# A 409.6 MB score matrix in wider stores: memory by parts of 1024 rows in groups of six

## The chip, the cores and the metric

The kernel runs on one core of one Trainium2 chip. The metric is the device time of a run in microseconds, median of several runs. Before the change it is 1660.91 us (three runs, 1660.71 to 1662.82). A separate run under the hardware profiler took 1589.44 us; all views below are of that run, whose span from the first to the last instruction is 1587.5 us.

## The reference

1024 sequences of 50 item numbers select rows of an embedding table of 100001 x 128 floats (row 0 counts as zero). Running means over time are normalised over the batch, drive a spiking neuron for 50 steps, and the mean spike rate is multiplied with the whole table:

```python
e = emb[seq]                                   # 1024 x 50 x 128
prefix = jnp.cumsum(e, axis=1)
denom = jnp.minimum(t_idx[None, :], lengths[:, None])
uF = prefix / denom[:, :, None]
y = (uF - uF.mean(axis=0)) * lax.rsqrt(uF.var(axis=0) + BN_EPS) * gamma + beta
def step(v, x):
    v = v + (x - v) / TAU                      # TAU = 2
    spike = atan_spike(v - V_TH)               # 1 where v >= 1
    v = v - lax.stop_gradient(spike) * V_TH
    return (v, spike)
_, spikes = lax.scan(step, v0, x_seq)
uF_out = spikes.mean(axis=0)                   # 1024 x 128
scores = uF_out @ emb.T                        # 1024 x 100001 floats, 409.6 MB
```

## The kernel before

There are two stages. In the first, GpSimd gathers 1024 table rows for each of 50 steps, and the other engines turn, normalise and integrate them; the table's first rows are loaded beside that. The result is the spike counts, `counts[n]`, eight blocks of 128 sequences. In the second, the table is worked through in chunks of 4096 rows, each of four parts of 1024 rows. A part is transposed on TensorE, split in two halves of reduced precision (`hi`, `lo`) by ScalarE and VectorE, multiplied with each of the eight blocks, evicted from PSUM in turn by VectorE and ScalarE into an output tile of 16 KB per partition, and stored.

The load of a chunk; eight chunks (32 parts) are loaded at the start from the SP queue, later ones from the ScalarE queue:

```python
CH = 4096
AHEAD = 8
HALF = 1024
...
def fetch(c, pool):
    engine = nc.sync if c < AHEAD else nc.scalar
    c0, w = chunks[c]
    r = pool.tile([P, CH // P, D], F32, tag="rows", name=f"rows_{c}")
    whole = w // HALF
    if whole:
        engine.dma_start(
            out=r[:, : whole * KQ, :].rearrange("p (q k) d -> p q (k d)", q=whole),
            in_=table[c0 : c0 + whole * HALF, :].rearrange("(q p k) d -> p q (k d)", p=P, k=KQ),
        )
    ...
```

Transposing and splitting a part, the product, the store:

```python
def turned(c, q, pt):
    ...
    for k0 in range(0, hw, P):
        nc.tensor.transpose(pt[:, k0 : k0 + kw], rows[c][:kw, q * KQ + k0 // P, :], ident[:kw, :kw])

def upper(c, q, pt):
    ...
    nc.scalar.copy(vh, vp)

def lower(c, q, pt):
    ...
    nc.vector.tensor_tensor(vl, vp, vh.bitcast(F32), ALU.subtract)

def product(po, c, q, n, k0, kw):
    for j, part in enumerate(split[c, q][:2]):
        nc.tensor.matmul(po[:, :kw], lhsT=counts[n], rhs=part[:, k0 : k0 + kw], start=j == 0, stop=j == 1)

def store(n, c0, o):
    nc.sync.dma_start(out=out[n * P : (n + 1) * P, c0 : c0 + o.shape[1]], in_=o)
```

The second stage (block 0 of the first chunk is done while the first stage ends):

```python
op = ctx.enter_context(tc.tile_pool(name="o", bufs=3, reuse_waits="tile"))
...
for c, (c0, w) in enumerate(chunks):
    todo = [(c + 1, q) for q in range(parts[c + 1])] if c + 1 < len(chunks) else []

    def ready():
        if todo and free:
            i, q = todo.pop(0)
            prepare(i, q, psum.tile([P, HALF], F32, tag="ps", name=f"pt_{i}_{q}"))

    for n in range(NB):
        ...
        o = op.tile([P, CH], F32, tag="o", name=f"o_{c}_{n}")
        for q in range(parts[c]):
            ...
            po = psum.tile([P, HALF], F32, tag="ps", name=f"po_{c}_{n}_{q}")
            for k0 in range(0, hw, BANK):
                product(po[:, k0 : k0 + BANK], c, q, n, k0, min(BANK, hw - k0))
            if turn % 2 == 0:
                nc.vector.tensor_scalar_mul(o[:, h0 : h0 + hw], po[:, :hw], 1.0 / T)
            else:
                nc.scalar.mul(o[:, h0 : h0 + hw], po[:, :hw], 1.0 / T)
            turn += 1
            ...
            if n == NB - 1:
                free.append(split.pop((c, q))[2])
                ready()
        if c or n > 1:
            store(n, c0, o[:, :w])
        if n in (2, 5):
            ready()
    if c + 2 == AHEAD:
        more = extrap.tile([P, 4, HALF], F32R, tag="rows", name="more")
        free += [(None, (more[:, i, :], more[:, i + 1, :])) for i in (0, 2)]
    elif ahead:
        fetch(ahead.pop(0), rowp)
```

`free` is the list of places for split parts: four at first, a fifth when the second stage begins, seven from the seventh chunk on.

Of the kernel before, what the change touches and what calls it, by code (L numbers as in the profile page):

```python
# [12 lines left out]
F32 = mybir.dt.float32  # L13
# [7 lines left out]
P = 128  # L21
BN_EPS = 1e-5
V_TH = 1.0
CH = 4096
AHEAD = 8
HALF = 1024
KQ = HALF // P
BANK = 512


@with_exitstack
def rec_kernel(
# [17 lines left out]

    const = ctx.enter_context(tc.tile_pool(name="const", bufs=1))
    embp = ctx.enter_context(tc.tile_pool(name="embT", bufs=1))
    rowp = ctx.enter_context(tc.tile_pool(name="rows", bufs=AHEAD - 2))

    extrap = ctx.enter_context(tc.tile_pool(name="extra", bufs=1))


    countA = const.tile([P, P], F32R, tag="countA", name="countA")
# [6 lines left out]

    chunks = [(c0, min(CH, N - c0)) for c0 in range(0, N, CH)]
    rows = {}
    split = {}  # L70
    parts = [-(-w // HALF) for _, w in chunks]

    free = [(embp, i) for i in range(4)]

    def fetch(c, pool):

        engine = nc.sync if c < AHEAD else nc.scalar
        c0, w = chunks[c]
        r = pool.tile([P, CH // P, D], F32, tag="rows", name=f"rows_{c}")
        whole = w // HALF  # L80
        if whole:
            engine.dma_start(
                out=r[:, : whole * KQ, :].rearrange("p (q k) d -> p q (k d)", q=whole),
                in_=table[c0 : c0 + whole * HALF, :].rearrange("(q p k) d -> p q (k d)", p=P, k=KQ),
            )
        c1 = c0 + whole * HALF
        full, rest = divmod(w - whole * HALF, P)
        k0 = whole * KQ
        if full:
            engine.dma_start(  # L90
                out=r[:, k0 : k0 + full, :],
                in_=table[c1 : c1 + full * P, :].rearrange("(k p) d -> p k d", p=P),
            )
        if rest:
            engine.dma_start(out=r[:rest, k0 + full, :], in_=table[c1 + full * P : c0 + w, :])
        rows[c] = r

    def turned(c, q, pt):
        hw = min(HALF, chunks[c][1] - q * HALF)
        if c == 0 and q == 0:  # L100
            nc.vector.memset(rows[c][0:1, 0, :], 0.0)
        for k0 in range(0, hw, P):
            kw = min(P, hw - k0)
            nc.tensor.transpose(pt[:, k0 : k0 + kw], rows[c][:kw, q * KQ + k0 // P, :], ident[:kw, :kw])  # L104

    def slot(c, q):
        place = free.pop(0)
        pool, i = place
        if pool is None:
            hi, lo = i  # L110
        else:
            hi = pool.tile([P, HALF], F32R, tag=f"hi{i}", name=f"hi_{c}_{q}")
            lo = pool.tile([P, HALF], F32R, tag=f"lo{i}", name=f"lo_{c}_{q}")
        split[c, q] = hi, lo, place
        return hi, lo

    def views(c, q, pt, hi, lo):
        hw = min(HALF, chunks[c][1] - q * HALF)
        if hw < HALF:
            return pt[:, :hw], hi[:, :hw], lo[:, :hw]  # L120
        return (
            pt.rearrange("d (k p) -> d p k", k=KQ),
            hi.rearrange("d (p k) -> d p k", k=KQ),
            lo.rearrange("d (p k) -> d p k", k=KQ),
        )

    def upper(c, q, pt):
        hi, lo = slot(c, q)  # L130
        hw = min(HALF, chunks[c][1] - q * HALF)
        if hw % 2:
            nc.vector.memset(hi[:, hw : hw + 1].bitcast(F32), 0.0)
            nc.vector.memset(lo[:, hw : hw + 1].bitcast(F32), 0.0)
        vp, vh, vl = views(c, q, pt, hi, lo)
        nc.scalar.copy(vh, vp)  # L136

    def lower(c, q, pt):
        vp, vh, vl = views(c, q, pt, *split[c, q][:2])
        nc.vector.tensor_tensor(vl, vp, vh.bitcast(F32), ALU.subtract)  # L140

    def prepare(c, q, pt):
        turned(c, q, pt)
        upper(c, q, pt)
        lower(c, q, pt)

    def product(po, c, q, n, k0, kw):
        kw += kw % 2  # L150
        for j, part in enumerate(split[c, q][:2]):
            nc.tensor.matmul(  # L152
                po[:, :kw],
                lhsT=counts[n],
                rhs=part[:, k0 : k0 + kw],
                start=j == 0,
                stop=j == 1,
            )
# [3 lines left out]


    with ExitStack() as ph:
        row0p = ph.enter_context(tc.tile_pool(name="rows0", bufs=1))
        once = ph.enter_context(tc.tile_pool(name="once", bufs=1))
        lp = ph.enter_context(tc.tile_pool(name="lif", bufs=2))
        sp = ph.enter_context(tc.tile_pool(name="stats", bufs=3))
# [11 lines left out]
        gb = once.tile([P, 2], F32, tag="gb", name="gb")  # L180
        nc.sync.dma_start(out=gb[:, 0:1], in_=gamma.rearrange("(d o) -> d o", o=1))
        nc.sync.dma_start(out=gb[:, 1:2], in_=beta.rearrange("(d o) -> d o", o=1))
        for c in range(min(AHEAD, len(chunks))):
            fetch(c, row0p if c == 0 else extrap if c == AHEAD - 1 else rowp)

        es = {}

# [99 lines left out]
        for t in range(T):  # L287
# [62 lines left out]
            if not last:  # L350
# [5 lines left out]
                if t + 2 < T:  # L356
                    l = only(t + 2)

                if T - 8 <= t < T - 2 and t % 2 == 0:
                    q = (t - T + 8) // 2  # L360
                    prepare(0, q, vp.tile([P, HALF], F32, tag="v1", name=f"pt_{q}"))

        pt = vp.tile([P, HALF], F32, tag="v0", name="pt_3")
        turned(0, 3, pt)
        x(halves[0])
        x(halves[1])
        upper(0, 3, pt)
        step(halves[0])  # L370
        spiked(countA, slice(0, P), vt)


        o = gp.tile([P, HALF], F32, tag="e", name="o_0_0_0")
        for h, po in enumerate(pre):
            product(po, 0, 0, 0, h * BANK, BANK)
        step(halves[1])
        nc.scalar.mul(o[:, :BANK], pre[0], 1.0 / T)
        store(0, 0, o[:, :BANK])
        lower(0, 3, pt)  # L380
        nc.vector.tensor_scalar_mul(o[:, BANK:], pre[1], 1.0 / T)
        store(0, BANK, o[:, BANK:])
        spiked(countB, slice(P, BANK), vt)
        spiked(countC, halves[1], vt)
        for q in range(1, 4):
            pool, tag = (gp, "e") if q == 1 else (up, "uF")
            o = pool.tile([P, HALF], F32, tag=tag, name=f"o_0_0_{q}")
            if q == 1:
                po = sums
            else:  # L390
                po = vp.tile([P, HALF], F32, tag=f"v{(q + 1) % 2}", name=f"po_0_0_{q}")
                po = [po[:, cs] for cs in halves]
            for h, cs in enumerate(halves):
                product(po[h], 0, q, 0, h * BANK, BANK)
            nc.scalar.mul(o[:, :BANK], po[0], 1.0 / T)
            nc.vector.tensor_scalar_mul(o[:, BANK:], po[1], 1.0 / T)
            store(0, q * HALF, o)

    embp2 = ctx.enter_context(tc.tile_pool(name="embT2", bufs=1, reuse_waits="tile"))
    op = ctx.enter_context(tc.tile_pool(name="o", bufs=3, reuse_waits="tile"))
    psum = ctx.enter_context(
        tc.tile_pool(name="psum", bufs=4, space=bass.MemoryType.PSUM, reuse_waits="tile")
    )
    free.append((embp2, 4))
    turn = 0
    ahead = list(range(AHEAD, len(chunks)))

    for c, (c0, w) in enumerate(chunks):
        todo = [(c + 1, q) for q in range(parts[c + 1])] if c + 1 < len(chunks) else []

        def ready():
            if todo and free:
                i, q = todo.pop(0)
                prepare(i, q, psum.tile([P, HALF], F32, tag="ps", name=f"pt_{i}_{q}"))

        for n in range(NB):
            if c == 0 and n == 0:  # L420
                continue
            if c + 1 < len(chunks):
                o = op.tile([P, CH], F32, tag="o", name=f"o_{c}_{n}")
            else:

                o = rowp.tile([P, CH], F32, tag="rows", name=f"o_{c}_{n}")
            for q in range(parts[c]):
                h0 = q * HALF
                hw = min(HALF, w - h0)
                po = psum.tile([P, HALF], F32, tag="ps", name=f"po_{c}_{n}_{q}")  # L430
                for k0 in range(0, hw, BANK):
                    product(po[:, k0 : k0 + BANK], c, q, n, k0, min(BANK, hw - k0))
                if turn % 2 == 0:
                    nc.vector.tensor_scalar_mul(o[:, h0 : h0 + hw], po[:, :hw], 1.0 / T)  # L434
                else:
                    nc.scalar.mul(o[:, h0 : h0 + hw], po[:, :hw], 1.0 / T)  # L436
                turn += 1
                if c == 0 and n == 1 and q % 2:
                    store(n, c0 + h0 - HALF, o[:, h0 - HALF : h0 + HALF])
                if n == NB - 1:  # L440
                    free.append(split.pop((c, q))[2])
                    ready()
            if c or n > 1:
                store(n, c0, o[:, :w])
            if n in (2, 5):
                ready()
        assert not todo
        if c + 2 == AHEAD:
            more = extrap.tile([P, 4, HALF], F32R, tag="rows", name="more")
            free += [(None, (more[:, i, :], more[:, i + 1, :])) for i in (0, 2)]  # L450
        elif ahead:
            fetch(ahead.pop(0), rowp)


# [17 lines left out]
```

## Time and profile before

| | |
|---|---|
| time, median of 3 | 1660.91 us |
| profiled span | 1587.5 us |
| mean granted TensorE clock | 0.954 |
| HBM read / written | 77.69 MB / 409.60 MB |
| stores of 2048 KB | 190, median 12.8 us from issue to landing |
| loads of 2048 KB on the ScalarE queue | 16, median 27.0 us to landing |
| ScalarE evictions that waited for a store to land | 347.4 us in 134 waits |
| VectorE evictions that waited for a store to land | 338.5 us in 136 waits |

How to read the views quoted below: a page gives each engine's busy time with its share of the span; then the span in 40 slices, in which a digit is the busy share in tenths; then the DMA queues (q1 is the SP queue's, q10 the ScalarE queue's, q0 the gathers') with packets, megabytes and the share of 16 DMA engines' time; then the chain of work that ended last, as shares of the span. An eviction that waits for a store costs nothing by itself: it shows that the output tiles are full, and the question is what the stores wait for.

### The profile page before, as it was taken

To read this page: it belongs to the slowest core of one execution; us is meant where nothing else is said; L and a number is where in the kernel's file an instruction comes from. 1 tells how busy PE (TensorE), PEld (TensorE's weight loads), DVE (VectorE), ACT (ScalarE), POOL (GpSimd) and SP (SyncE) were. 2 spreads that over 40 slices of the span, in tenths; PEclk is the share of its full clock that TensorE was granted. 3 is DMA by queue.
4 is the path that set the end of the run, shared out by engine and by line. 5 is a ranking of instruction groups with operands and counts; after the bars stand their busy time and mean duration, and the time that the engine had idled before them with its cause. 6 is when DMAs were issued, how large, how long until landed. Compare 5 with 4: busy or idle time off the path is not lost.

```text
span 1587.5 us, 12689 instructions
## 1 busy us (share of the span) xinstructions
PE 1137.8 (72%) x4532; PEld 804.7 (51%) x4532; DVE 939.4 (59%) x1162; ACT 631.6 (40%) x699; POOL 378.4 (24%) x406
## 2 busy tenths in 40 slices
PE   4555555555555977788888878788888788888884
PEld 2222222222233765566666666666666666666663
DVE  4777777777778654555555554555555545555553
ACT  2322222222233544444444444444444444444442
POOL 6777777777775000000000000000000000000000
PEclk9999999999965999999999999999999999999998
DMA  9522122221221999999999999999999999999998
GB/s 341 187 53 53 52 53 53 53 53 52 53 53 51 380 429 426 424 422 415 418 426 407 418 426 422 417 414 415 416 416 419 422 420 411 427 411 412 416 417 345
DMA packets 58410, 488.13 MB, mean 307 GB/s; under 512 B 12491, under 2 KB 13292, under 8 KB 33772
## 3 DMA queue, kind: packets, MB, share of 16 engines
q1 hardware_dynamic: 36256, 426.67, 63.9%
q0 software_dynamic: 12800, 26.24, 6.1%
q10 hardware_dynamic: 9292, 34.42, 6.1%
q8 instruction: 35, 0.57, 0.1%
q14 instruction: 27, 0.22, 0.0%
HBM read 77.69 MB, written 409.60 MB: 307 GB/s over the span
## 4 chain that ended last, share of the span: by engine, by line
DMA 52%; POOL 18%; issue 10%; PE 9%; DVE 7%; ACT 3%; DVEq 0%; SPq 0%; ACTq 0%; POOLq 0%
DMA scores<-o 48%; POOL e L191 18%; PE po L152 8%; DVE o L434 5%; DMA e<-in_L_rec_emb_table,idx 3%; ACT o L436 3%; PE pt L104 1%; PE pre L300 0%; ACT hi L136 0%; DVE s L330 0%; DVE bs L310 0%; DVE uF L309 0%; DMA idx<-in_r_seq 0%; ACT v L345 0%; DVE negv L353 0%
## 5 line engine op out<-in xcount | busy, mean ns | idle before, releaser
L434 DVE TENSOR_SCALAR o<-po 128x1024 f32<-128x1024 f32 x390 | 462.6, 1220 | 442.0 <-DMA scores<-o 338.5
L436 ACT ACTIVATE o<-po 128x1024 f32<-128x1024 f32 (+1 forms) x390 | 385.4, 1018 | 528.2 <-DMA scores<-o 347.4
L191 POOL DMA_INDIRECT e<-in_L_rec_emb_table,idx x400 | 377.7, 944 | 124.6 <-issue 116.4
L152 PE MATMUL po<-hi,countC 128*128 128x512 f32 x624 | 261.0, 418 | 81.7 <-ACT o L436 81.5
L300 PE MATMUL pre<-ident,e 128*128 128x128 f32 x400 | 155.9, 451 | 146.9 <-DMA e<-in_L_rec_emb_table,idx 145.0
L152 PE MATMUL po<-lo,countC 128*128 128x512 f32 x624 | 248.9, 399 | 0.0
L152 PE MATMUL po<-hi,countB 128*128 128x512 f32 x468 | 192.2, 411 | 14.4 <-ACT o L436 13.9
L300 PEld LDWEIGHTS pre<-ident,e 128*128 128x128 f32 x400 | 79.2, 200 | 241.7 <-DMA e<-in_L_rec_emb_table,idx 219.9
L152 PEld LDWEIGHTS po<-hi,countC 128*128 128x128 f32 x624 | 120.2, 193 | 133.5 <-ACT o L436 110.7
L152 PE MATMUL po<-lo,countB 128*128 128x512 f32 x468 | 186.9, 399 | 0.0
L104 PE MATMUL pt<-ident,rows 128*128 128x128 f32 x782 | 113.2, 292 | 70.5 <-ACT o L436 65.4
L104 PEld LDWEIGHTS pt<-ident,rows 128*128 128x128 f32 x782 | 96.4, 150 | 96.3 <-ACT o L436 79.8
L324 ACT ACTIVATE r<-mv,eps 128x1 f32<-128x1 f32 x50 | 14.8, 295 | 302.8 <-DVE mv L320 302.8
L152 PEld LDWEIGHTS po<-lo,countC 128*128 128x128 f32 x624 | 120.5, 193 | 22.1
L309 DVE SCALAR_TENSOR_TENSOR uF<-rlen,pre 128x512 f32<-128x512 f32 x100 | 68.3, 683 | 105.5 <-PE pre L300 105.5
L140 DVE TENSOR_TENSOR lo<-pt,hi 128x1024 fp32r<-128x1024 f32 x78 | 93.7, 1218 | 40.9 <-ACT hi L136 40.9
L152 PEld LDWEIGHTS po<-hi,countB 128*128 128x128 f32 x468 | 91.6, 196 | 41.7 <-ACT o L436 19.8
L152 PEld LDWEIGHTS po<-lo,countB 128*128 128x128 f32 x468 | 91.1, 195 | 18.2
L152 PE MATMUL po<-more,countC 128*128 128x512 f32 (+1 forms) x320 | 87.7, 413 | 16.1 <-ACT o L436 16.1
L136 ACT CAST hi<-pt 128x1024 fp32r<-128x1024 f32 x78 | 79.0, 1013 | 48.7 <-PE pt L104 48.7
L268 PE MATMUL sums<-s,ident_h 128*128 128x512 bf16 x98 | 49.6, 608 | 61.1 <-DVE s L330 61.1
L257 PE MATMUL pre<-zT,l 128*128 128x512 f32 x100 | 76.9, 771 | 19.7 <-DVE uF L309 19.5
(77 smaller groups left out, 942.7 us busy)
## 6 DMA issues: line engine op xcount, KB each, us to landing
scores<-o SPq DMA_DIRECT2D x190, 2048.0 KB, 12.8
rows<-in_L_rec_emb_table ACTq DMA_DIRECT2D x16, 2048.0 KB, 27.0
rows<-in_L_rec_emb_table SPq DMA_DIRECT2D x8, 2048.0 KB, 26.0
scores<-o SPq DMA_DIRECT2D x8, 848.5 KB, 14.6
e<-in_L_rec_emb_table,idx POOLq DMA_INDIRECT x400, 2.5
scores<-o SPq DMA_DIRECT2D x2, 1024.0 KB, 3.9
scores<-o SPq DMA_DIRECT2D x3, 512.0 KB, 2.7
scores<-o SPq DMA_DIRECT2D x2, 256.0 KB, 2.1
```

The costliest lines, as they stand in the source:

```text
L104: nc.tensor.transpose(pt[:, k0 : k0 + kw], rows[c][:kw, q * KQ + k0 // P, :], ident[:kw, :kw])
L136: nc.scalar.copy(vh, vp)
L140: nc.vector.tensor_tensor(vl, vp, vh.bitcast(F32), ALU.subtract)
L152: nc.tensor.matmul(po[:, :kw], lhsT=counts[n], rhs=part[:, k0 : k0 + kw], start=j == 0, stop=j == 1,)
L191: nc.gpsimd.indirect_dma_start(out=es[t][:, n * P : (n + 1) * P], out_offset=None, in_=table, in_offset=bass.IndirectOffsetOnAxis(ap=idx[: ...
L257: nc.tensor.matmul(pre[h], lhsT=l, rhs=zT[:, h * BANK : (h + 1) * BANK], start=t == 0, stop=False, skip_group_check=True,)
L268: nc.tensor.matmul(sums[h], lhsT=ident_h, rhs=s[:, h * BANK : (h + 1) * BANK], start=t == 0, stop=t == T - 2, skip_group_check=True,)
L300: nc.tensor.matmul(pre[h][:, k : k + P], lhsT=e[:, h * BANK + k : h * BANK + k + P], rhs=ident, start=False, stop=last, is_transpose=True, ...
L309: nc.vector.scalar_tensor_tensor(uF[:, cs], rlen[:, cs], 1.0 / (t + 1), pre[h], ALU.max, ALU.mult)
L324: nc.scalar.activation(r, mv[:, 1:2], AF.Sqrt, bias=eps)
L434: nc.vector.tensor_scalar_mul(o[:, h0 : h0 + hw], po[:, :hw], 1.0 / T)
L436: nc.scalar.mul(o[:, h0 : h0 + hw], po[:, :hw], 1.0 / T)
```

## The change

The unit of memory becomes the part of 1024 rows instead of the chunk of 4096. Loads come in groups of six parts; six groups (36 parts instead of 32) are brought in during the first stage. The second stage's chunks are 2, 2, 2, 3, 3, 3, 3, then twelve times 6, then 4, 4 parts wide. Memory that earlier groups leave becomes places for split parts (ten in the end, instead of seven) and output tiles (three of 24 KB per partition instead of three of 16 KB). It is for longer rows in each store, for fewer loads beside the stores, and for more room to split parts ahead of their use. The diff, cut to what matters:

```diff
-CH = 4096
-AHEAD = 8
+GROUP = 6
+AHEAD = 6
+
+WIDTHS = [2, 2, 2, 3, 3, 3, 3] + 12 * [6] + [4, 4]
+NARROW, MIDDLE = 3, 7
...
+    free = [
+        [embp.tile([P, HALF], F32R, tag=f"{x}{i}", name=f"{x}_{i}") for x in ("hi", "lo")] for i in range(2)
+    ]
+    def group(g):
+        at = g if g < AHEAD else AHEAD - 2 + g % 2
+        r = rowp.tile([P, GROUP, HALF], F32, tag=f"rows{at}", name=f"rows_{g}")
+        for k in range(GROUP):
+            rows[g * GROUP + k] = r[:, k, :]
+        return r
...
-        for c in range(min(AHEAD, len(chunks))):
-            fetch(c, row0p if c == 0 else extrap if c == AHEAD - 1 else rowp)
+        for g in range(AHEAD):
+            fetch(group(g), g * GROUP, GROUP)
...
-                if T - 8 <= t < T - 2 and t % 2 == 0:
+                if t in (T - 8, T - 6):
...
-        pt = vp.tile([P, HALF], F32, tag="v0", name="pt_3")
-        turned(0, 3, pt)
         x(halves[0])
         x(halves[1])
-        upper(0, 3, pt)
...
+    def places(at):
+        t = rowp.tile([P, GROUP, HALF], F32R, tag=f"rows{at}", name=f"pairs_{at}")
+        free.extend((t[:, k, :], t[:, k + 1, :]) for k in range(0, GROUP, 2))
+
+    for c, W in enumerate(WIDTHS):
+
+        if c in (0, NARROW, MIDDLE):
+            opening.close()
+            where = opening if c < MIDDLE else ctx
+            op = where.enter_context(tc.tile_pool(name="o", bufs=1, reuse_waits="tile"))
+            if c == 0:
+                third = [op.tile([P, HALF], F32R, tag=x, name=x) for x in ("hi2", "lo2")]
+                free.append(third)
+                turns = [(op, f"o{k}", 2) for k in range(4)]
+            elif c == NARROW:
+                assert third in free
+                free.remove(third)
+                turns = [(op, f"o{k}", 3) for k in (2, 0, 1)]
+            else:
+                fourth = op.tile([P, 4, HALF], F32R, tag="pairs", name="pairs")
+                free.extend((fourth[:, k, :], fourth[:, k + 1, :]) for k in (0, 2))
+                turns = [(rowp, "rows2", 6), (rowp, "rows3", 6), (op, "o", 6)]
+            blocks = 0
...
         def ready():
-            if todo and free:
-                i, q = todo.pop(0)
-                prepare(i, q, psum.tile([P, HALF], F32, tag="ps", name=f"pt_{i}_{q}"))
+            nonlocal to_split
+            if to_split < q2 and free:
+                prepare(to_split, psum.tile([P, HALF], F32, tag="ps", name=f"pt_{to_split}"))
+                to_split += 1
+
+                if to_split in (GROUP, 2 * GROUP):
+                    places(to_split // GROUP - 1)
...
-            if n in (2, 5):
+                store(n, q0 * HALF, o[:, : min(N, q1 * HALF) - q0 * HALF])
+            if 2 <= n < NB - 1:
                 ready()
...
-        elif ahead:
-            fetch(ahead.pop(0), rowp)
+            if n in (1, 4) and c >= MIDDLE and to_fetch < parts:
+                g = to_fetch // GROUP
+                if to_fetch % GROUP or to_split >= (g - 1) * GROUP:
+                    if to_fetch % GROUP == 0:
+                        r = group(g)
+                    fetch(r, to_fetch, GROUP // 2)
+                    to_fetch += GROUP // 2
```

## The prediction

> **What bounds the kernel now.** I read the page from the top: the shares of the engines, the slices over time, the DMA queues, the chain that ended last; then busy time by stage; then the chain inside a stretch without loads.
>
> ```profile
> PE 1137.8 (72%) x4532; PEld 804.7 (51%) x4532; DVE 939.4 (59%) x1162; ACT 631.6 (40%) x699; POOL 378.4 (24%) x406
> ...
> DMA  9522122221221999999999999999999999999998
> GB/s 341 187 53 53 52 53 53 53 53 52 53 53 51 380 429 426 424 422 415 418 426 407 418 426 422 417 414 415 416 416 419 422 420 411 427 411 412 416 417 345
> ...
> q1 hardware_dynamic: 36256, 426.67, 63.9%
> ...
> q10 hardware_dynamic: 9292, 34.42, 6.1%
> ...
> DMA 52%; POOL 18%; issue 10%; PE 9%; DVE 7%; ACT 3%; DVEq 0%; SPq 0%; ACTq 0%; POOLq 0%
> ```
>
> No engine is above 72%. There are two stages. For 504 us GpSimd issues 400 gathers, eight per step, back to back, and the DMA is 20% busy. From about 522 us to 1580 us the DMA rows read 9: 409.6 MB of scores and 34.4 MB of loads pass in about 1,060 us, some 418 GB/s. This is the stage the change touches.
>
> By stage (columns: window, its length, busy us of PE, PEld, DVE, ACT, POOL, granted clock, DMA share, GB/s):
>
> ```profile
> 514.00:522.00 8.00, 6.85 (x28) 5.02 (x27) 5.26 (x8) 2.82 (x4) 0.00 (x0) 0.97 0.67 262
> 522.00:532.00 10.00, 10.00 (x49) 8.34 (x48) 7.14 (x7) 6.04 (x6) 0.00 (x0) 1.00 0.94 392
> 700.00:800.00 100.00, 80.71 (x356) 62.77 (x355) 50.85 (x45) 42.74 (x44) 0.00 (x0) 0.95 1.01 419
> 1400.00:1432.00 32.00, 27.25 (x128) 21.00 (x127) 16.58 (x14) 14.94 (x16) 0.00 (x0) 1.00 1.00 424
> 1436.00:1440.00 4.00, 4.00 (x19) 3.29 (x18) 3.56 (x4) 2.31 (x3) 0.00 (x0) 1.00 0.77 315
> ```
>
> The DMA share is 1.0 almost everywhere. It dips only at chunk borders late in the run (0.77 over 4 us here), six times, about 5 us in all.
>
> ```profile
> 1389.70 12.67 DMA scores<-o
> ...
> 1404.91 12.69 DMA scores<-o
> ...
> 1420.14 12.60 DMA scores<-o
> ```
>
> This is the chain from 1396 to 1442 us (start, length). A store needs 12.7 us to land and three are in flight. The semaphore events of these stores give the true beat: they are complete at 1427.65, 1432.73, 1437.80, 1442.87 and 1447.94 us, one per 5.07 us, with no gap at the dip. Of the 16 increments of a store, 13 arrive within 0.4 us, the 15th 2 us and the last 5 us after the first. So one DMA engine runs a whole store behind, and a buffer is free only when that engine is through. The dip is the other engines waiting for it. Total time of stage two is the packets of the slowest engine.
>
> The trace's packet records (size, duration) price this. Median durations of stores: 2,048 B 86 ns, 4,096 B 161 ns (by the fit), 8,192 B 311 ns, 16,384 B 611 ns. The line through the last two is 11 ns + 36.6 ns per 1,000 B, and it gives the 86 ns of the first. Loads of 4,096 B take 159 ns. A whole 16 KB row is one packet, eight per engine and store. The slow engine's beat, 5.07/8 = 633 ns, is 22 ns above the median.
>
> **What the Trainium skill says.** "DMA: Bandwidth & Descriptors", section "Queues, rings and completion order": a copy is split over up to 16 engines whose semaphore increments come independently, and queues alternate by packets. The trace agrees: 16 increments spread over 5 us. Its section "Latency and other measured facts" says engines 7 and 15 are usually slower than the others; the trace has stragglers (the last three increments) but does not number them. Its section "Rules for kernel authors" asks for at least 1 MiB per DMA and 128 partitions; the stores are already 2 MB, so this rule promises nothing for 3 MB. Its section "Why small descriptors are slow" names a fixed overhead per packet; the fit's 11 ns are such a term, and they are the only thing that longer rows can save.
>
> **The change, part by part.**
>
> 1. Store packets. Before: 190 stores of 16 KB rows, 8 of 6.8 KB, 7 smaller ones, 205 in all, so 205 x 8 = 1,640 packets per engine. After, counted in the program's order: 2 of 2 KB rows, 3 of 4 KB, 22 of 8 KB, 32 of 12 KB, 96 of 24 KB, 16 of 16 KB or a little less: 171 stores, 1,368 packets per engine. Bytes are the same. Saved: 272 packets. At the 11 ns of the fit that is 3.0 us. If the slow engine's 22 ns extra are also per packet, 272 x 33 ns = 9.0 us. The narrow first chunks (8 and 12 KB rows for 18 of 98 parts) eat a good part of what 24 KB rows bring.
>
> 2. Loads. 36 parts instead of 32 are brought in under the gather stage, where the DMA is 20% busy and GpSimd never waits for it. So 4 x 128 rows = 512 packets leave stage two, 32 per engine, at 159 ns: 5.1 us. A second way: a chunk with a 2 MB load lasts 45.1 us by the landings, one without 40.5 us: 4.6 us. I take 4.8 us.
>
> 3. The gather stage keeps its length: its first loads grow by 2.1 MB (about 5 us of DMA around 46 us), but GpSimd issued its gathers without a pause through the same crowd before (0.30 us between them, always "issue"). Splitting two parts instead of three inside it and none after it takes 8 transposes (1.9 us of PE), one ScalarE copy (1.0) and one VectorE subtraction (1.2) off the hand-over; but the first store goes out at 513.5 us behind counts, products and one eviction, and those items lay in gaps beside that path. Worth 0.
>
> 4. Opening of stage two. Before, the DMA lacked about 0.33 x 8 = 2.6 us between 514 and 522 us. After, a part-block (one part, one block of 128 sequences) still costs PE four products at 0.23 us, 0.92 us, against 5.07/4 = 1.27 us on the DMA, so PE gains a lead of 0.35 us each. But the first extra split now falls in block 2, when six part-blocks are done instead of twelve, and with it 8 transposes (0.9 us PE). Finer stores of 0.5 and 1 MB offset this. 0 to +1.5 us; I take +0.7.
>
> 5. Buffers. Three 24 KB output tiles: a fill takes 6 x 0.92 = 5.5 us plus one split (0.9 us PE) while two other stores hold 2 x 7.6 us. No wait there. Ten places mean four of the six next splits happen in blocks 2 to 5 and two in block 7; before, two to three fell in block 7. That removes the dips, which by the above were not on the path: 0.
>
> Sum: -3 to -9 (middle -6) - 4.8 + 0.7 = about -10 us of profiled time, 1587.5 to about 1577 us. The timed runs are 1660.9 us where the profiled one has 1589.4; the 71.5 us between them are not in any view, so I carry them over: 1651 us.
>
> **Rivals.** (a) The dips are on the path after all: another -5 us, 1646. For it: the DMA share does fall. Against: the landings keep their 5.07 us beat through it. (b) The slow engine is slow per byte, not per packet: item 1 shrinks to 3 us, 1654. Its 633 against 611 ns cannot tell. (c) The unseen 71.5 us are DMA time, for instance more per packet: if all of it sat on the 1,640 packets, 43 ns each, item 1 would gain 272 x 43 ns = 12 us more, 1639. Nothing in the profile speaks for or against it. (d) A new wait: at chunk 3 the output tiles are laid over older ones, and the first 12 KB tile waits for the store of block 5 of the chunk before; two 1 MB stores (5 us) then cover a fill of about 3.5 us. Or loads, which start only at chunk 8 and are 62 parts in 11 chunks, come late: 24 load packets alternating with 24 KB store packets need about 24 x 1.08 = 26 us, and have 60. Each such wait would cost 2 to 10 us, 1653 to 1661; I hold it unlikely.
>
> **Range and chances.** The additive terms give 1646 to 1656; (c) stretches the low side, (d) and the unseen 71.5 us the high side: 1635 to 1666. Two per cent is 33 us, below 1628 or above 1694. The first needs (a), (c) and the good end of item 1 together, 0.09; the second a stall at nearly every chunk, 0.03.
>
> **What would show it.** Right: no store packets of 16 KB before the last two chunks but 24,576 B ones near 911 ns, q10 near 32.3 MB, stores of 3 MB landing every 7.4 to 7.55 us where no loads run, and one increment still far behind the rest. Item 1 is at its good end if that beat is 7.46 us or less, at its poor end near 7.55. Wrong: 24 KB rows recorded as two packets (item 1 turns to a loss), idle DMA between 520 and 545 us of more than 4 us, PE transposes waiting for loads, or a gather stage that ends later than 504 us.

## The result and the profile after

| | before | after | ratio after/before, 95% interval |
|---|---|---|---|
| time, median | 1660.81 us (4 runs, 1660.06 to 1662.82) | 1653.2 us (4 runs, 1650.76 to 1653.55) | 0.9949, 0.9932 to 0.9966 |

The kernel is 0.5% faster: 7.6 us by the medians, against a predicted 10 us. The predicted time was 1651 us, its range 1635 to 1666.

From the page of the kernel after (engines with busy us and share of the span; the slices; the queues; the chain that ended last):

```profile
PE 1105.9 (67%) x4522; PEld 824.5 (50%) x4532; DVE 940.6 (57%) x1161; ACT 629.7 (38%) x698; POOL 378.2 (23%) x406
...
DMA  9511111111111169999999999999999999999898
GB/s 345 208 44 48 48 48 43 48 47 47 48 43 46 39 285 411 416 422 396 430 423 429 431 425 431 419 416 425 431 426 412 417 419 416 427 426 422 371 426 365
...
q1 hardware_dynamic: 31840, 428.77, 61.7%
...
q10 hardware_dynamic: 8844, 32.33, 5.0%
...
DMA 46%; DVE 23%; PE 11%; another core or an unknown queue 10%; ACT 5%; issue 4%; DVEq 0%; ACTq 0%; SPq 0%
```

Two things are to be seen. Queue q10 carries 32.33 MB instead of 34.42: these are the four parts that are no longer loaded beside the stores. And this profile, with a span of 1651.7 us, cannot be laid beside the 1587.5 us of before as it stands: the stretch of low DMA digits reaches to slice 14 of a longer span (slices of 41.3 instead of 39.7 us), the share of GpSimd in the chain is gone, and DVE with "another core or an unknown queue" has come in. The gather stage of this execution is some 62 us longer. So I cut every profile at the issue of its first store and compare the two parts by themselves. All figures are us; the last column is the median of the kernel before in the timed runs on the same chip.

| execution | last gather issued | first store issued | from there to the end | before on that chip |
|---|---|---|---|---|
| before, as in the prediction | 502.6 | 513.5 | 1074.0 | 1660.8 |
| after | 565.0 | 587.8 | 1063.9 | 1660.8 |
| before, again (first experiment) | 502.4 | 513.1 | 1074.0 | 1589.5 |
| before, once more (seventh) | 565.1 | 584.6 | 1074.5 | 1657.9 |
| after, again (seventh) | 564.9 | 582.3 | 1064.9 | 1657.9 |

The first stores of before and of after, in the SP queue's view (start, time that the merged issues span, what):

```profile
513.47 1.31 SPq L161 DMA_DIRECT2D scores<-o  x2
587.81 1.31 SPq L158 DMA_DIRECT2D scores<-o  x2
```

The stage of the stores takes 1074.0 to 1074.5 us before and 1063.9 to 1064.9 after, whatever the gather stage does: 10.1 and 9.6 us less. That is where the change lies. The timed runs show 7.6 us of it; experiment 7 takes up the rest.

Busy time by stage of the kernel after (columns as in the prediction: window, length, PE, PEld, DVE, ACT, POOL, granted clock, DMA share, GB/s):

```profile
588.00:596.00 8.00, 8.00 (x37) 6.43 (x36) 5.27 (x7) 3.55 (x4) 0.00 (x0) 0.88 0.75 295
596.00:606.00 10.00, 9.74 (x48) 7.71 (x47) 8.12 (x8) 6.10 (x6) 0.00 (x0) 1.00 0.92 377
1100.00:1200.00 100.00, 83.48 (x355) 65.75 (x356) 52.80 (x45) 43.84 (x45) 0.00 (x0) 0.91 1.00 423
...
1548.00:1556.00 8.00, 6.11 (x21) 4.55 (x20) 3.58 (x3) 2.96 (x3) 0.00 (x0) 0.79 0.34 143
1600.00:1632.00 32.00, 25.00 (x109) 20.00 (x110) 15.39 (x14) 10.72 (x13) 0.00 (x0) 1.00 1.01 423
```

The opening lacks 0.25 x 8 + 0.08 x 10 = 2.8 us of DMA, against 0.33 x 8 + 0.06 x 10 = 3.2 us before. The bulk runs at share 1.0 and 423 GB/s, against 419 in the window of before. New is the hole between 1548 and 1556 us, where the DMA is busy a third of the time.

The chain of work of the kernel after around that hole (start, length, what):

```profile
1500.55 19.15 DMA scores<-o
...
1532.07 18.27 DMA scores<-o
...
1560.44 17.46 DMA scores<-o
...
1580.45 12.72 DMA scores<-o
```

The 3 MB stores issued at 1500 and 1532 us are 18 to 19 us in flight (12.7 us for 2 MB before). The one at 1560 us is already a 2 MB store of the last chunks, issued behind two of 3 MB; from 1580 us on a 2 MB store takes 11 to 13 us again. The semaphore events give the beat: three successive 3 MB stores are complete at 1542.71, 1550.34 and 1557.89 us, 7.63 and 7.55 us apart. The last increment still comes far behind, 8.1 to 8.6 us after the first. The beat goes through the hole undisturbed, as it went through the dips before: the store issued at the end of the hole, at 1554.89 us, is complete at 1565.39, 7.50 us after the one before it.

The packet records have 12,288 store packets of 24,576 B with a median of 912 ns, so a 24 KB row is one packet. They do not number the engines; for the slow one, which finishes last, the beat gives 7.55/8, about 944 ns each.

### The profile page after: what moved, and what is told of

The parts are those of the page before. It is cut to its first block, busy times and chain, and to the rows that moved or that the text cites. A ratio compares the mean times of both kernels' runs of the same rounds, so it can differ in the third digit from the quotient of the medians.

```text
span 1651.7 us, 12520 instructions
## 1 busy us (share of the span) xinstructions
PE 1105.9 (67%) x4522; PEld 824.5 (50%) x4532; DVE 940.6 (57%) x1161; ACT 629.7 (38%) x698; POOL 378.2 (23%) x406
## 3 DMA queue, kind: packets, MB, share of 16 engines
q10 hardware_dynamic: 8844, 32.33, 5.0%
## 4 chain that ended last, share of the span: by engine, by line
DMA 46%; DVE 23%; PE 11%; another core or an unknown queue 10%; ACT 5%; issue 4%; DVEq 0%; ACTq 0%; SPq 0%
DMA scores<-o 46%; PE po L149 9%; ACT o L447 4%; DVE bs L306 4%; DVE uF L305 4%; DVE v L344 4%; DVE s L326 3%; DVE negv L349 3%; DVE o L445 2%; DVE a L335 1%; DVE mv L316 1%; PE pt L119 1%; DVE q L332 0%; DVE q L331 0%
## 5 line engine op out<-in xcount | busy, mean ns | idle before, releaser
L149 PE MATMUL po<-pairs,countC 128*128 128x512 f32 x1168 | 316.3, 416 | 60.6 <-ACT o L447 60.4
L149 PEld LDWEIGHTS po<-pairs,countC 128*128 128x128 f32 x1168 | 224.2, 198 | 121.2 <-ACT o L447 75.4
L149 PE MATMUL po<-pairs,countB 128*128 128x512 f32 x876 | 234.1, 414 | 52.7 <-ACT o L447 37.1
L253 PE MATMUL pre<-zT,l 128*128 128x512 f32 x100 | 71.5, 717 | 256.5 <-DVE uF L305 217.4
L149 PEld LDWEIGHTS po<-pairs,countB 128*128 128x128 f32 x876 | 169.3, 198 | 101.9 <-ACT o L447 48.3
L142 DVE TENSOR_TENSOR pairs<-pt,pairs 128x1024 fp32r<-128x1024 f32 (+1 forms) x73 | 88.4, 1217 | 95.3 <-ACT pairs L141 95.1
L149 PE MATMUL po<-hi,countC 128*128 128x512 f32 x200 | 85.2, 426 | 18.6 <-ACT o L447 18.4
L149 PE MATMUL po<-lo,countC 128*128 128x512 f32 x200 | 82.3, 411 | 0.0
L149 PE MATMUL po<-pairs,countA 128*128 128x512 f32 (+1 forms) x292 | 74.1, 396 | 9.5 <-ACT o L447 9.4
L141 ACT CAST pairs<-pt 128x1024 fp32r<-128x1024 f32 (+1 forms) x73 | 73.5, 1007 | 15.9 <-PE pt L119 15.8
L341 ACT ACTIVATE v<-uF,hgb,a 128x1024 f32<-128x1024 f32 (+1 forms) x51 | 60.8, 1192 | 37.6 <-DVE a L335 19.5
```

The costliest lines, as they stand in the source:

```text
L253: nc.tensor.matmul(pre[h], lhsT=l, rhs=zT[:, h * BANK : (h + 1) * BANK], start=t == 0, stop=False, skip_group_check=True,)
```

## The experiments

Each kernel differs from the changed one by the edit shown, where nothing else is said. "Stage" is the time from the first issued store to the end, 1063.9 us in the changed kernel.

### 1. The kernel before, unchanged: where are the 71.5 us?

> The kernel before, unchanged, profiled again. Theory (the 71.5 us that separate the first profile of it, 1589 us, from its timed runs, 1661 us, lie in the gather stage): the first store leaves at about 585 us instead of 513 us, the mean granted clock is near 0.80 instead of 0.954, and the store stage from the first store to the end again takes about 1074 us. Rival (they lie in the store stage, as slower packets): first store at about 513 us again, store stage about 1145 us, 16 KB packets near 655 ns instead of 611 ns.

Measured: 1589.23 us. On this chip the kernel before needs 1589.46 us (median of 17 runs, 1588.39 to 1590.32) and never 1660. Its first store is issued at 513.1 us although the mean granted clock is 0.818; between 40 and 500 us it is only 0.51, and still a step takes 10.0 us. So the low clock that the theory expected beside a long gather stage came without one: it does not lengthen that stage by itself. Where the 71.5 us lie could not be seen here and had to wait for a chip that has them (experiment 7).

### 2. Stores split by columns: what does a packet cost?

```diff
-                store(n, q0 * HALF, o[:, : min(N, q1 * HALF) - q0 * HALF])
+                if W == GROUP:
+                    for k in range(0, GROUP, 2):
+                        store(n, (q0 + k) * HALF, o[:, k * HALF : (k + 2) * HALF])
+                else:
+                    store(n, q0 * HALF, o[:, : min(N, q1 * HALF) - q0 * HALF])
```

> The kernel after, with each 24 KB-row store issued as three stores of 8 KB rows (96 stores become 288; the same tiles, products and bytes; 96 x 2 x 8 = 1,536 more packets per DMA engine). Theory A (every packet costs a fixed 11 ns, and 9 ns for each added completion): +16.9 + 1.7 = about +19 us. Theory B (the slowest engine pays 33 ns per packet): +51 + 2 = about +53 us. Theory C (cost goes by bytes alone, row length does nothing): within 3 us.

Measured: 1604.73 us, ratio to before 1.0097 (1.0082 to 1.0113); stage 1089.2 us, 25.3 longer. The DMA issues (operation, count, KB each, median us to landing):

```profile
scores<-o SPq DMA_DIRECT2D x310, 1024.0 KB, 17.2
```

Each of the 96 large stores became three: 192 more stores, each with an increment that the packet records put at 9 ns per engine, 1.7 us, and 1,536 more packets per engine. (25.3 - 1.7)/1536 = 15.4 ns for a packet. That is nearer to the 11 ns of the fit than to the 33 ns that the good end of item 1 needed.

### 3. No loads in the second stage: what does a part's load cost?

```diff
...
-        r = rowp.tile([P, GROUP, HALF], F32, tag=f"rows{at}", name=f"rows_{g}")
+        if g < AHEAD:
+            kept[g] = rowp.tile([P, GROUP, HALF], F32, tag=f"rows{at}", name=f"rows_{g}")
+        r = kept[at]
...
-                    fetch(r, to_fetch, GROUP // 2)
```

The scores of parts 36 to 97 are computed from table rows that are already there, so they are those of other rows; work and stores are the same.

> The kernel after without any load in the store stage: parts 36 to 97 are taken from rows already held, so their scores are those of other table rows; all products, evictions and stores are kept. If a part's load costs 1.16 us of store time (from the chunk beats of the kernel before: 11.29 us per part with loads, 10.13 without), 62 parts make -72 us. If loads overlap the stores and cost less than their packets (62 x 8 x 159 ns = 79 us of every engine), -40 us or less. The wait of one store for the last small loads (see the next run) goes as well, another -5.

Measured: 1506.98 us, ratio 0.9482 (0.9468 to 0.9497); stage 991.8 us, 72.1 less. Of its page, the queue of the stores, which now has no q10 beside it:

```profile
q1 hardware_dynamic: 31840, 428.77, 67.7%
```

The loads of sixty-two parts less give 72.1 us: 1.16 us for each part, and 4.65 us for the four that the change brings in earlier. The loads are not hidden beside the stores, they are added to them. This run also shows the beat where no loads run, from end to end of the wide chunks: the 24 KB stores are complete every 7.53 us.

### 4. The last load in large packets: does the hole of 8 us cost anything?

The hole has a cause that can be followed in the semaphore events. The store of block 6 in the last six-part chunk had its tile filled by 1547.1 us and was issued only at 1554.89. Its completion counter is also that of another transfer: the load of the last 640 rows, issued at 1507.19 us in 640 packets of 512 B, which had not landed before 1554.82. The edit loads these rows as 128 packets of 2,560 B, and the split takes them in their new order:

```diff
-                    in_=table[c1 : c1 + full * P, :].rearrange("(k p) d -> p k d", p=P),
+                    in_=table[c1 : c1 + full * P, :].rearrange("(p k) d -> p k d", k=full),
...
```

> The kernel after, with the last part's 640 whole-tile rows loaded as five neighbouring rows per partition (128 packets of 2,560 B, 8 per engine) instead of 640 packets of 512 B (40 per engine, one between every two 24 KB store packets). Theory: in the kernel after that load took some 47 us and a store that shares its completion counter waited for it from about 1547 to 1554.8 us, with the DMA engines idle for 5 us; this gives -5 us, and the idle stretch is gone. Rival (the stretch is the end of a chunk with its splits, not the load): within 1 us, and the idle stretch stays.

Measured: 1579.32 us, ratio 0.9937 (0.9923 to 0.995); stage 1063.7 us.

```profile
rows<-in_L_rec_emb_table ACTq DMA_DIRECT2D x1, 320.0 KB, 20.0
```

The load now lands in 20.0 us instead of 47.6, the hole is gone (one of 2 us opens later, at 1500 us), and the end does not move. In the hole most engines are idle while the slow one works through, as the beat shows; filling it gives nothing. So idle DMA engines beside a busy last one were free here, which speaks against rival (a) of the prediction.

### 5. Splits later, as before: are the ten places worth something?

```diff
-            if 2 <= n < NB - 1:
+            if n in (2, 5) or c < MIDDLE and 2 <= n < NB - 1:
```

> The kernel after, with parts split ahead only in blocks 2 and 5 of each six-part chunk and the other four in block 7, as the kernel before did, so that the extra places go unused. Theory (idle stretches of the fast DMA engines at chunk borders cost nothing, since the slowest engine works through them): within 2 us of the kernel after's -10 us against the kernel before, though the DMA share dips at the borders. Rival (the dips are lost time and the early splits earned part of the gain): 5 to 15 us slower than the kernel after.

Measured: 1653.61 us, ratio 0.9952 (0.9936 to 0.9969), as the change itself; stage 1063.3 us. The dips at the borders are back. A stretch at one border, in this run and in the changed kernel:

```profile
1093.00:1095.00 2.00, 2.00 (x10) 1.66 (x9) 2.00 (x3) 1.03 (x1) 0.00 (x0) 1.00 0.09 37
1093.00:1095.00 2.00, 2.00 (x10) 1.66 (x9) 1.46 (x3) 1.26 (x2) 0.00 (x0) 1.00 0.96 406
```

The DMA share is 0.09 instead of 0.96. Yet the two stores that complete after this dip, at 1099.26 and 1106.79 us, come 7.58 and 7.53 us after the ones before them. The even spacing of the splits, and with it the additional places, is worth nothing in this stage. Item 5 is confirmed, and rival (a) is out.

### 6. TensorE kept busy in the gather stage

Two products with a tile of zeros after each transpose of a gathered tile, to hold the granted clock up (and the load of experiment 4):

```diff
...
+                    if 2 <= t < T - 1:
+                        for _ in range(WARM):
+                            nc.tensor.matmul(
+                                sums[h], lhsT=zero[:, :P], rhs=zero, start=False, stop=False, skip_group_check=True
+                            )
```

> The kernel of the short tail load, with two multiplications by zero (bf16, 512 columns, into the count sums) after each of the eight transposes of a step, to keep TensorE busy in the gather stage; they add zero to the result. On a chip where the kernel before takes about 1660 us, theory (there TensorE drops its clock in the gather stage and the steps come as 19, 7.5, 7.5 us): steps of 10 us again and 60 to 70 us less. On a chip where the kernel before takes about 1589 us its steps are 10 us already, as GpSimd's eight gathers take 10 us: within 3 us of the kernel after. Rival (the long steps have another cause): steps of 19 us stay.

Measured: 1664.38 us against 1660.52 of the kernel before, ratio 1.0019 (1.0011 to 1.0027). Busy time in the gather stage:

```profile
40.00:500.00 460.00, 281.65 (x1088) 149.57 (x1109) 284.19 (x513) 112.29 (x158) 300.09 (x319) 0.80 0.22 62
```

The clock there rose to 0.80 (0.54 in the first profile of the changed kernel), and the first store came at 599.7 us, 12 us later than the 587.8 of experiment 5 on the same chip. The steps come neither every 10 us, as the theory said, nor as 19, 7.5 and 7.5 us, as the rival said, but irregularly, most of them 9 to 15 us apart. So a higher clock did not make this stage shorter. As the added products take time of TensorE themselves, the run does not tell what the clock alone would do. The stage of the stores takes 1064.9 us.

### 7. Before and after on a chip with the long gather stage

Both kernels unchanged.

> The kernel before, unchanged, for a look at its stages on whatever chip this is. Theory: the 71.5 us between its profile (1587.5 us) and its timed runs (1660.9 us) are a longer gather stage. If this chip is one that times it near 1660, the first store is issued at 584 to 588 us instead of 513, the steps of the gather stage come 19, 7.5 and 7.5 us apart instead of 10, and the stage of the stores still takes 1074 us. If it times it near 1589, the first store is issued at 513. Rival: the stage of the stores is the longer one, near 1145 us.

> The changed kernel, unchanged, beside the kernel before on one chip. Theory: the change is worth the same 10 us on any chip, because it lies in the stage of the stores alone: stage of the stores 1063.9 us, and the time 1579 us where the kernel before has 1589, or 1651 to 1653 where it has 1660. Rival: some 2.5 us of it are given back in a gather stage that ends later with the new placement: then on a chip where the kernel before needs 1660, its first store comes near 585 and this one's near 588.

Measured: before 1657.94 us (24 runs), after 1648.98 us (5 runs, 1643.15 to 1651.18), ratio 0.993 (0.9907 to 0.9954). In the profile of before the first store is issued at 584.6 us and the stage takes 1074.5 us: the 71.5 us lie wholly ahead of the stores, and the change has no part in them. After has 582.3 and 1064.9 us. The rival of 2.5 us given back before the stores stays open. In this pair the change is 2.3 us earlier, but these are single profiles. From the last gather to the first store the new placement takes 17.4 us here and 22.4 to 23.0 us in six other profiles with the long gather stage (the first one of the change and those of experiments 5, 6, 8 and 9), against 19.5 us in the only such profile of the kernel before. With the short gather stage it takes 10.7 to 10.9 us in every profile, before and after. So with the long stage some 3 us of the gain can be lost before the first store, which would make the 7.6 us of the first result out of 10.1.

What the gather stage waits for, in the groups of instructions between 100 and 500 us (busy us, mean ns, then idle before and its releaser). The kernel before in the execution of 1587.5 us:

```profile
L309 DVE SCALAR_TENSOR_TENSOR uF<-rlen,pre 128x512 f32<-128x512 f32 x80 | 54.6, 683 | 85.5 <-PE pre L300 85.5
```

The same kernel in this execution:

```profile
L191 POOL DMA_INDIRECT e<-in_L_rec_emb_table,idx x285 | 268.9, 943 | 132.6 <-issue 81.7 <-remote 50.1 <-DMA e<-in_L_rec_emb_table,idx 0.9
...
L309 DVE SCALAR_TENSOR_TENSOR uF<-rlen,pre 128x512 f32<-128x512 f32 x70 | 47.6, 680 | 132.7 <-remote 130.1 <-issue 2.6
```

And one of its long steps, on VectorE (start, length, instruction, idle time before it):

```profile
300.56 0.67 DVE L309 SCALAR_TENSOR_TENSOR uF<-rlen,pre 128x512 f32<-128x512 f32 x1
301.99 0.21 DVE L320 BATCH_NORM_AGGREGATE mv<-bs 128x2 f32<-128x12 f32 x1
311.55 0.69 DVE L309 SCALAR_TENSOR_TENSOR uF<-rlen,pre 128x512 f32<-128x512 f32 x1 [4.74 <-remote]
318.54 0.69 DVE L309 SCALAR_TENSOR_TENSOR uF<-rlen,pre 128x512 f32<-128x512 f32 x1 [5.57 <-remote]
319.99 0.21 DVE L320 BATCH_NORM_AGGREGATE mv<-bs 128x2 f32<-128x12 f32 x1
```

From one batch statistic to the next 18.0 us pass, where the short stage has 10.0; the step after it takes 7.5 us. Over the fifty steps the last gather comes 62.5 us later (565.1 against 502.6), 1.25 us per step in the mean, and the hand-over after it takes 19.5 us instead of 10.9: together the 71 us. VectorE waits for a semaphore that only TensorE's instructions raise. It rises at 311.53 us, just before VectorE goes on at 311.55, while the records put the last transpose of this step at 307.5 us; GpSimd then waits 3.3 us for the same semaphore. So TensorE's signal is late; why, and why only on some chips, stays open. A low clock is excluded as the cause by itself (experiment 1).

### 8. The new placement with stores of four parts

```diff
-WIDTHS = [2, 2, 2, 3, 3, 3, 3] + 12 * [6] + [4, 4]
+WIDTHS = [2, 2, 2, 3, 3, 3, 3] + [6] + 17 * [4] + [6]
```

> The new placement with 36 parts held, but the wide chunks of four parts, 16 KB stores, as before (one of six, then seventeen of four, one of six). 320 store packets per engine more than with six parts, 1,688 instead of 1,368. Theory (15.4 ns per packet, from the run with split stores, and 40 stores more at some 9 ns): the stage of the stores takes 1069 us, 5 us longer than 1063.9. Rival one, a packet costs nothing beyond its bytes: 1064. Rival two, 33 ns per packet, from the median packets of 11 and 33 ns in the prediction: 1074.5.

Measured: 1656.26 us, ratio 0.9984 (0.9977 to 0.9992); stage 1069.5 us. The stores by size:

```profile
scores<-o SPq DMA_DIRECT2D x136, 2048.0 KB, 14.2
scores<-o SPq DMA_DIRECT2D x32, 1536.0 KB, 9.5
scores<-o SPq DMA_DIRECT2D x8, 3072.0 KB, 15.6
```

The stage was to be 1069 us at 15.4 ns per packet, 1064 at nothing and 1074.5 at 33 ns. With the 0.36 us for 40 more stores taken off, 320 packets cost 5.2 us against the first profile of the change (16 ns each) and 4.2 us against the second (13 ns). The six-part chunks are worth 4.6 to 5.6 us over four-part ones, which the packets and stores account for at the price of experiment 2.

### 9. Fewer rows in a store: 120, 112, and twice 64

The slow engine suggested a store that spares an engine. In every chunk, wide or narrow, 120 rows of each block are stored; 8 rows are left unwritten (only the first five stores are whole).

```diff
...
-                store(n, q0 * HALF, o[:, : min(N, q1 * HALF) - q0 * HALF])
+                store(n, q0 * HALF, o[:120, : min(N, q1 * HALF) - q0 * HALF])
```

> The kernel after, but each store of the second stage from the second chunk on writes only 120 of a block's 128 rows (8 rows of each block of scores are left unwritten); tiles, products, evictions and loads are kept. By the Trainium skill, page DMA: Bandwidth & Descriptors, such a store goes to 15 engines, 8 rows each, and the highest-numbered engine gets none. Theory (one DMA engine, slower than the rest by about 4% per byte, sets the time, and it is the last one): the beat of a 24 KB store falls from 7.55 to about 7.27 us and the store stage from 1064 by 25 to 35 us. Rival 1 (the slow engine is another): every other engine has as many packets as before, within 3 us. Rival 2 (no engine is special, the whole memory path is the limit and 1/16 fewer bytes come through it): 15/16 of the store time, -60 us.

Measured: 1834.41 us in the median of four runs that spread from 1709 to 1871; the profile is of a run of 1807 us, with a stage of 1216.6 us. It fell against every expectation: 6% fewer bytes took 14% longer there, and even the fastest of the four runs is 55.5 us above the 1653.6 of experiment 5 on the same chip.

```profile
1000.00:1100.00 100.00, 74.73 (x308) 58.99 (x309) 48.55 (x41) 39.09 (x40) 0.00 (x0) 0.90 0.93 338
```

The DMA share of 0.93 is near 15/16, as if one engine had no stores. The Trainium skill says so on the page "DMA: Bandwidth & Descriptors", section "Why a DMA increments its semaphore by 16 and not by 1": the number of engines is the largest one up to 16 that divides the rows, and the unused ones' increments are written at once. The trace agrees: about 15 packets are in flight at a time, and one increment of a store issued at 1220.37 us is there at 1220.87, the next at 1230.62. But the fifteen are not undisturbed: the 24 KB packets keep a median of 912 ns, while their mean is 1,089 ns and a tenth of them takes 1.7 us or more.

By the same rule 112 rows make sixteen engines of seven rows (16 rows of each block unwritten; in the narrow chunks too, not only in the wide ones):

> Stores of 112 of the 128 rows in the wide chunks; 16 rows of each block are left unwritten, so the output is not complete. It asks why stores of 120 rows, over fifteen engines, took longer. Theory: what costs is that the rows fall on fewer than sixteen engines: if 112 rows go to fourteen engines of eight rows, the engines drift apart as there and the stage of the stores takes over 1100 us, with 24 KB packets far above 912 ns in the mean. Rival: 112 rows are spread as sixteen times seven; then all engines stay in step, the packets stay near 915 ns, and the stage takes 7/8 of its store time, near 945 us.

Measured: 1847.54 us (one run); stage 1260.3 us. Up to sixteen packets are in flight at once and no increment comes ahead, so it is sixteen times seven, as the rival said. Yet the packets have a mean of 1,143 ns, so the rival's 945 us did not come either: the theory's time did, without its reason. Then all 128 rows, in two stores of 64 from row `p0` on:

```diff
...
-                store(n, q0 * HALF, o[:, : min(N, q1 * HALF) - q0 * HALF])
+                for p0 in (0, P // 2) if W == GROUP else (0,):
+                    rows_ = slice(p0, p0 + (P // 2 if W == GROUP else P))
+                    store(n, q0 * HALF, o[rows_, : min(N, q1 * HALF) - q0 * HALF], p0)
```

> All 128 rows are stored, but each 24 KB store goes out as two of 64 rows: the same 1,368 packets per engine, 96 more stores, four rows per engine and store instead of eight. It asks what made stores of 120 and of 112 rows slow (24 KB packets of 912 ns in the median but 1,089 and 1,143 in the mean). Theory one: engines that carry other rows than their eight of 128 (seven in the run with 112 rows, four here) get in each other's way; then the packets have a mean over 1,000 ns here too and the stage of the stores takes over 1,150 us. Theory two: it comes from rows of a block that no store covers; then it is gone: packets of 923 ns in the mean and a stage of about 1065 us (1063.9 and some 9 ns for each store more).

Measured: 1891.8 us (one run, beside 1589.24 of the kernel before); stage 1376.3 us, 312 us more than with whole stores.

```profile
scores<-o SPq DMA_DIRECT2D x224, 1536.0 KB, 21.1
...
1000.00:1100.00 100.00, 69.09 (x270) 54.22 (x268) 38.05 (x33) 32.08 (x33) 0.00 (x0) 0.83 0.92 293
```

The same 12,288 packets of 24 KB now have a mean of 1,234 ns; 36% of them take over 1.3 times the median. The narrow chunks of the same run, whose stores have 128 rows, are undisturbed (8 KB packets: mean 317 ns, as in the changed kernel). So unwritten rows are not needed for it. The outcome is that of theory one, but its reason is not shown: with 120 rows the fifteen engines carry eight rows each, as they do with 128, and are slow too. What is shown is that stores of these kernels run at full rate with all 128 rows and not with 120, 112 or 64; with one run each for 112 and 64 and a wide spread for 120, an order among the three is not shown. Why the packets stretch stays open; the trace does not tell which engine or which memory a packet met. One rival stands untested: a store of fewer rows also reads fewer partitions of the output tile at once, and no run varies which partitions these are while the count of rows stays. And whether sparing the slow engine would pay could not be seen this way.

## Why the prediction was right, point by point

**Item 1, packets: right in its mechanism, its middle too high.** I put 11 to 33 ns on each of 272 packets and took the middle, 6 us. Experiments 2 and 8 give 15.4 and 13 to 16 ns. A third way is the beats where no loads run: 5.06 us for 16 KB stores before, 7.53 us for 24 KB stores (experiment 3), or 633 and 941 ns for a packet of the slow engine; the line through these two has 17 ns at no bytes. So the item is worth 3.5 to 4.6 us, in the lower half of its range. The beat said the same: it was to be 7.46 us or less at the good end and near 7.55 at the poor end. Rival (b), that the slow engine is slow per byte, holds in the main: where no loads run, its 633 ns stand against a median of 615 at 16 KB and its 941 against 916 at 24 KB, a ratio of 1.03 in both, while the difference grew from 18 to 25 ns. That the rival's time of 1654 us lies beside the measured 1653.2 is no proof of it, since some 3 us ahead of the stores can be in that time (experiment 7). The overhead per packet exists, as the Trainium skill's page "DMA: Bandwidth & Descriptors" says in "Why small descriptors are slow (HBM only)"; it works it out for 256 B, and here it is seen between 8 and 24 KB.

**Item 2, loads: right.** 4.65 us by experiment 3, against 4.8.

**Item 3, gather stage: right up to the last gather, open after it.** The last gather is issued at 565.1 us before and 564.9 after on one chip. From there to the first store nothing changed in the short stage (10.7 to 10.9 us); in the long stage, which I had not seen, the change may lose some 3 us (experiment 7).

**Item 4, opening: not seen.** 2.8 us of DMA are missing in it, against 3.2 before; I had put +0.7 us on it. No run tries it by itself.

**Item 5, buffers: right.** Experiment 5 puts the early splits at nothing. The hole at 1548 us, a store held back by a shared completion counter, was not foreseen, and cost nothing (experiment 4).

**The sum.** Loads 4.65, packets 3.5 to 4.6, and 34 stores fewer at about 9 ns, 0.3: 8.5 to 9.6 us. The stage lost 10.1 and 9.6. Up to 1.6 us are not accounted for by any run; profiles of one kernel differ by up to 1.0 us in this stage. That the stage lost so nearly the predicted 10 us is in part luck: a too large item 1 and a loss in item 4 that did not show cancelled. In the timed runs the gain was 7.6 and 9.0 us.

**The 71.5 us carried over: right, for a reason I did not have.** They are the gather stage of some chips, before and after nearly alike, so carrying them over was sound, which no view had shown: that was luck. Rival (c), that they are DMA time on the packets, is out: the stage of the stores is 1074.0 and 1074.5 us with and without them. My sign "a gather stage that ends later than 504 us" was a bad sign: it came true in the profile of after (565.0 us), and says only which chip it ran on. Rival (d), new waits on the path, did not occur: where the wide chunks begin the DMA share falls to 0.65 between 768 and 772 us, but the stores there are complete 3.83, 7.58 and 7.86 us apart, the beats of 12 and 24 KB rows, without a gap.

## What to carry to other kernels

When a stage is bound by the DMA, price a change by what it takes off the engine that ends last: here a load moved out of the stage was worth nearly its packet time (1.16 us per 512 KB part, whose eight packets per engine take 8 x 159 ns = 1.27 us), a wider store only about 15 ns for each packet saved, and idle time of the other engines nothing. Before comparing two profiles, cut them at the same event: two executions of one kernel differed by 71 us in a stage that the change did not touch. And measure before you store fewer than 128 rows at once: making a row longer or shorter moved the stage of these kernels by at most 2.4%, cutting the rows of a store by 14 to 29% in the profiled runs.

## What the runs showed of the hardware that was not expected

- A store of fewer than 128 rows ran slower per byte than a whole one: 24 KB packets of 923 ns in the mean with 128 rows, 1,089 with 120, 1,143 with 112 and 1,234 with 64.
- The gather stage comes in two lengths on different chips with the same program, with the first store at 513 or at 582 to 588 us (600 with the added products). In the short one the granted clock was 0.95 between 40 and 500 us in one execution and 0.51 in another, both with 10.0 us per step; in the long one the steps come irregularly, often as 18 to 19, 7.5 and 7.5 us.
- A load of 512 B packets beside 24 KB stores lands late: 640 packets took 47.6 us to land, and the same bytes as 128 packets of 2,560 B took 20.0 us. A store that shares its completion counter was held for 7.8 us.
